# Four graph layers on eight batches: where the next pair's norm stands in the TensorE order of layer 3

## The chip, the cores and the metric

The kernel runs on one core of one Trainium2 chip. The metric is the device time of one execution in microseconds (us), taken as the median of several runs. The profile is of one more execution of the same kernel; its durations belong to that execution, whose own time is given beside its span below.

## The reference, cut to what matters

The input x has 8 batches of 2048 nodes with 64 features; adj is a 2048 x 2048 matrix of zeros and ones. Four layers follow one another, each of the form x + layer(relu(layernorm(x))). Only layers 2 and 3 and the norm matter for this change:

```python
def _layernorm(x, axis=-1, eps=1e-5):
    m = jnp.mean(x, axis=axis, keepdims=True)
    v = jnp.var(x, axis=axis, keepdims=True)
    return (x - m) / jnp.sqrt(v + eps)
...
    for _ in range(MAX_STEPS):                       # layer 2, three steps
        effects = jnp.einsum('nm,bmd->bnd', adj_matrix, v)
        h = jnp.concatenate([v, effects], axis=-1)
        h = jax.nn.relu(jnp.einsum('bnk,dk->bnd', h, W1) + b1)
        v = jnp.einsum('bnk,dk->bnd', h, W2) + b2
...
    As = [jnp.eye(N, dtype=x.dtype)]                 # layer 3
    As.append(A)
    for _ in range(2, K):
        As.append(2.0 * (A @ As[-1]) - As[-2])
    x_g = jnp.einsum('knm,bmc->bnkc', A_stack, x)
    out = jnp.einsum('bnki,nkio->bno', x_g, w)
```

So layer 2 multiplies by the adjacency three times, layer 3 twice more, and layer 3 ends with one product per node, whose weights come from 16 stored matrices mixed by an embedding of the node.

## The kernel before, in words

**Tiling.** Two batches make a pair, so that 2 x 64 features fill 128 partitions; there are NP = 4 pairs, done one after the other. The 2048 nodes are NT = 16 tiles of P = 128, or NCW = 4 chunks of CW = 512; the last chunk has the number LAST = 3. The adjacency lies in SBUF for the whole time, as 16 tiles aT[m].

**Spread.** The product with the adjacency is the function spread: for one chunk of 512 nodes it accumulates over all 16 source tiles m, two matmuls for each (a high and a low part of the operand), into one PSUM tile acc: 32 matmuls. For each pair there are 20 spreads: three steps of layer 2 with four chunks, then four chunks for each of layer 3's two products with the adjacency.

**Layer 3's products.** After the second spread of a chunk, its result is copied to y2 (L2113), and then come the products of that chunk: for each of its four node tiles k and each half w of the 16 weight matrices, matmuls of the 64-row halves of v, y1 and y2 with W3 into u0 and u1, two PSUM buffers each. That is 96 matmul records per chunk, "64*128" in the profile. VectorE multiplies each u by the embedding (L2135), adds the two halves w (L2139) and folds (L2146); GpSimd folds on and adds the residual xr (L2147 to L2149); the result is stored by SyncE's queue (L2150).

**The norm.** normed is a layernorm with relu across partitions. It has two TensorE products with the averaging matrix, mean and var, and between them the subtraction on VectorE (L1974) and the Square on ScalarE (L1975); after var come Ln and Exp (L1979, L1980) and the scaling on VectorE (L1981). enter is the norm of one chunk of the next pair's input, followed by moved: four small products py with W1e and their split in two parts (L1954, L1955). The last chunk has no free place in v, so it is normed in places of y1 that are no longer read, and copied to v at the pair's end (L2155).

**leave** ends layer 2 for one chunk: the product pv with W2, the residual (L2018), four transposes tx, the norm of layer 3 along the free dimension on VectorE and ScalarE (L2029 to L2040, its cast on ScalarE being L2039), and later the transposes tv. Before it, ScalarE's relu (L2084) has turned acc into v; pv reads that v.

**What sets the order.** Matmuls and transposes are kept in the order in which the program issues them (mm and turn, with strict on). Instructions of the other engines, and the loads on SyncE's queue, are put in order by the scheduler of the framework, which can take a later one first if it expects it to be ready first. The program's own order is written by Weave, a planner with a clock of its own: a chain is a generator that yields the delay to its next step, and a spread calls passed(0.47) after each source tile m, the products call passed(2.8) after each (k, w), and the first product of a layer 2 chunk passed(0.93). A step is issued at the first such call at which its due time is reached:

```python
    def passed(self, us):
        self.now += us
        for c in list(self.chains):
            if c[0] <= self.now:
                self.step(c)
```

In layer 3's loop over c, the chain enter(c - 1) is started after the second spread of chunk c and after the copy to y2, with a delay of 0.0; so its steps fall among the products of chunk c. With c = LAST there are two chains, for chunks 2 and 3. The chunk of the next pair's input is loaded ahead of the spread of chunk c; fin's tag x has two buffers, one of which holds xr. The mean and var of these chains use the PSUM buffers of acc. The last pair has no next one and no such chains.

Of the kernel before, what the change touches and what calls it, by code (L numbers as in the profile page):

```python
# [19 lines left out]
NP = B // 2  # L20
# [11 lines left out]
def cols(c, w=CW):  # L32
    return slice(c * w, (c + 1) * w)
# [1865 lines left out]
def layers23(self, aT):  # L1899
# [69 lines left out]
    def normed(dst, src, tags, xc=None):  # L1969

        mean = ps.tile([P, CW], FP, tag=tags[0], name="mean")
        mm(mean, kit.avg, src, start=True, stop=True)
        xc = fin.tile([P, CW], FP, tag="ca", name="xc") if xc is None else xc
        nc.vector.tensor_sub(xc, src, mean)  # L1974
        nc.scalar.activation(dst, xc, AF.Square)  # L1975
        yield 3.5
        var = ps.tile([P, CW], FP, tag=tags[1], name="var")
        mm(var, kit.avg, dst, start=True, stop=True)
        nc.scalar.activation(dst, var, AF.Ln, bias=kit.eps)  # L1979
        nc.scalar.activation(dst, dst, AF.Exp, scale=-0.5)  # L1980
        nc.vector.scalar_tensor_tensor(dst, xc, 0.0, dst, op0=OP.max, op1=OP.mult)  # L1981
        yield 3.5

    def spread(acc, y, c, start, ms):

# [11 lines left out]
    def chunk_of(src, c):  # L1997
        return load(fin.tile([P, CW], FP, tag="x", name="xp"), src, c)
# [13 lines left out]

    def leave(p, c, xp, yn):

        yield 1.4
        pv = ps.tile([P, CW], FP, tag="tp", name="pv")
        mm(pv, W2, v[:, cols(c)], start=True, stop=True)
        nc.vector.scalar_tensor_tensor(xp, pv, b2c, xp, op0=OP.add, op1=OP.add)  # L2018
        bq = load(sb.tile([P, CW], FP, tag="pr", name="bq", bufs=3), kit.bias_dram, c)
        yield 1.8  # L2020

        tx = ps.tile([P, 4, P], FP, tag="u0", name="tx")
        for k in range(4):
            kit.turn(tx[:, k, :], xp[:, k * P : (k + 1) * P])
        nc.scalar.copy(xp, tx.rearrange("p k n -> p (k n)"))  # L2025
        groups = lambda a: a.rearrange("p (g f) -> p g f", f=F)
        spans = lambda a: a[:, :, None].to_broadcast([P, 8, F])
        st = sb.tile([P, 2, 8], FP, tag="st", name="st")
        nc.vector.tensor_reduce(st[:, 0], groups(xp), AX.X, OP.add)  # L2029
        vn = fin.tile([P, CW], FP, tag="ca", name="vn")  # L2030
        nc.vector.scalar_tensor_tensor(groups(vn), spans(st[:, 0]), -1.0 / F, groups(xp), op0=OP.mult, op1=OP.add)
        nc.scalar.activation(v[:, cols(c)], vn, AF.Square)
        nc.vector.tensor_reduce(st[:, 1], groups(v[:, cols(c)]), AX.X, OP.add)
        nc.scalar.activation(st[:, 1], st[:, 1], AF.Ln, bias=kit.eps, scale=1.0 / F)
        nc.scalar.activation(st[:, 1], st[:, 1], AF.Exp, scale=-0.5)
        nc.vector.scalar_tensor_tensor(groups(vn), groups(vn), 0.0, spans(st[:, 1]), op0=OP.max, op1=OP.mult)
        hi, lo = parts(LENT[c])
        flat = lambda a: a.rearrange("p k n -> p (k n)")
        nc.scalar.copy(flat(hi), vn)  # L2039
        nc.vector.tensor_tensor(flat(lo), vn, flat(hi).bitcast(FP), op=OP.subtract)  # L2040
        yn[c] = hi, lo
        nc.gpsimd.tensor_add(bq, bq, xp)  # L2042
        nc.sync.dma_start(out=x3_dram[p, :, cols(c)], in_=bq)
        yield 7.0
        tv = ps.tile([P, 4, P], FP, tag="u1", name="tv")
        for k in range(4):
            kit.turn(tv[:, k, :], vn[:, k * P : (k + 1) * P])
        nc.scalar.copy(v[:, cols(c)], flat(tv))

    def again(y1, c, yn):  # L2050
        yield 1.4
        yn[c] = turned(y1, c)
# [17 lines left out]
    for p in range(NP):  # L2070
        for step in range(3):
            yn = [None] * NCW
            if p == 0 and step:
                weights(step)
            for c in range(NCW):
                acc = ps.tile([P, CW], FP, tag="acc", name="acc")
                if step < 2:
                    got = raw(2)
                else:
                    xp = chunk_of(x2_dram[p], c)  # L2080
                mm(acc, Wvc if step else W1v, v[:, cols(c)], start=True, stop=False)
                weave.passed(0.93)
                spread(acc, y, c, False, every)
                nc.scalar.activation(v[:, cols(c)], acc, AF.Relu, bias=b1c if step else b1)  # L2084
                if step < 2:
                    check(got)
                weave.start(carry(c, step, yn) if step < 2 else leave(p, c, xp, yn))
            y = yn


        y1 = sb.tile([P, N], FP, tag="y1", name="y1", bufs=1)
        yn, after = [None] * NCW, [None] * NCW

        two = [ps.tile([P, CW], FP, tag="acc", name="acc") for c in range(2)]
        for ms in (range(0, 8), range(8, 12), range(12, NT)):
            for c in range(2):
                spread(two[c], y, c, 0 in ms, ms)
                if NT - 1 in ms:
                    nc.scalar.copy(y1[:, cols(c)], two[c])
                    weave.start(again(y1, c, yn))  # L2100
        for c in range(2, NCW):
            acc = ps.tile([P, CW], FP, tag="acc", name="acc")
            spread(acc, y, c, True, every)
            nc.scalar.copy(y1[:, cols(c)], acc)
            weave.start(again(y1, c, yn))
        for c in range(NCW):
            xr = chunk_of(x3_dram[p], c)
            acc = ps.tile([P, CW], FP, tag="acc", name="acc")
            if c > 0 and p + 1 < NP:
                xp = chunk_of(x2_dram[p + 1], c - 1)  # L2110
            spread(acc, yn, c, True, every)
            y2 = fin.tile([P, CW], FP, tag="ca", name="y2")
            nc.scalar.copy(y2, acc)  # L2113
            if c > 0 and p + 1 < NP:
                weave.start(enter(c - 1, after, xp, 0.0, ("acc", "acc")))
                if c == LAST:

                    xp = load(y1[:, cols(0)], x2_dram[p + 1], c)
                    weave.start(enter(c, after, xp, 2.0, ("acc", "acc"), y1))
            for k in range(4):  # L2120
                i = 4 * c + k
                ns, ks = slice(i * P, (i + 1) * P), slice(k * P, (k + 1) * P)
                pr = []
                for w in range(2):
                    u = [ps.tile([P, 8, F], FP, tag=f"u{h}", name=f"u{h}") for h in range(2)]
                    for kk, src in enumerate((v[:, ns], y1[:, ns], y2[:, ks])):
                        for h in range(2):

                            mm(
                                u[h].rearrange("p d o -> p (d o)"), src[half(h), :], W3[half(h), kk, cols(w)],  # L2130
                                start=kk == 0, stop=kk == 2,
                            )
                    for h in range(2):
                        a = sb.tile([P, 8, F], FP, tag="pr", name="pr", bufs=3)
                        nc.vector.tensor_tensor(  # L2135
                            a, u[h], emb[:, i, 8 * w : 8 * w + 8, None].to_broadcast([P, 8, F]), op=OP.mult
                        )
                        if w:
                            nc.vector.tensor_add(pr[h], pr[h], a)  # L2139
                        else:  # L2140
                            pr.append(a)
                    weave.passed(2.8)
                fold = sb.tile([P, 2, 4, F], FP, tag="fold", name="fold")
                ot = sb.tile([P, 2, F], FP, tag="ot", name="ot", bufs=1)
                for h in range(2):
                    nc.vector.tensor_add(fold[:, h], pr[h][:, 0:4, :], pr[h][:, 4:8, :])  # L2146
                nc.gpsimd.tensor_add(fold[:, :, 0:2, :], fold[:, :, 0:2, :], fold[:, :, 2:4, :])  # L2147
                nc.gpsimd.tensor_add(ot, fold[:, :, 0, :], fold[:, :, 1, :])
                nc.gpsimd.tensor_add(ot, ot, xr[:, ks].rearrange("p (h f) -> p h f", h=2))  # L2149
                nc.sync.dma_start(  # L2150
                    out=out[2 * p : 2 * p + 2, ns, :].rearrange("h p f -> p h f"), in_=ot
                )
        if p + 1 < NP:
            weave.until(lambda: None not in after)
            nc.scalar.copy(v[:, cols(LAST)], y1[:, cols(1)])  # L2155
        y = after
# [103 lines left out]
```

## Time and profile before

| what | value |
| --- | --- |
| median of 3 runs (lowest, highest) | 1966.83 us (1963.56, 1970.12) |
| the profiled execution: its own time, its span | 1963.12 us, 1961.3 us |
| busy in the span: TensorE, VectorE, ScalarE, GpSimd | 1900.6, 1190.7, 438.0, 315.4 us |
| granted TensorE clock, mean | 0.989 |
| layers 2 and 3 of the four pairs | from about 862 us to the end |
| records of mean and var of the norms that enter makes (two for each product) | 24 and 24 |
| times that the loading of pv's weights waited for ScalarE's L2084 | 12, together 6.8 us |

The span is the time from the first to the last instruction; the execution's own time is 1.82 us longer. "Busy" counts instructions, not waits, and TensorE's matmuls are pipelined, so a matmul's own duration is longer than the step from one to the next. The step is read from the chain of work that ended last: there, consecutive matmuls of one kind are merged into one line with their number, and the length of the line divided by the number is the step. One product in full fp32 with 512 columns shows as two records.

### The profile page before, as it was taken

The numbers are of one execution on the slowest core, as the hardware profiler recorded it, in microseconds if no ns is written. First come the engines' busy times: TensorE is split into PE (matmuls) and PEld (weight loads), VectorE is DVE, ScalarE is ACT, GpSimd is POOL, SyncE is SP. The second block draws the span as 40 slices with busy tenths as digits, with TensorE's granted clock in tenths as the row PEclk, the third lists the DMA queues.
The fourth block names the chain that finished last, engine by engine and source line by source line (L and its number), as shares of the span: only waits on it lengthen the run. The fifth ranks groups of instructions, "written<-read, shape, count | busy, mean of one in ns | idle before, by whom it ended". The sixth has DMA issues, their size and how long they took to land.

```text
span 1961.3 us, 23490 instructions
## 1 busy us (share of the span) xinstructions
PE 1900.6 (97%) x9060; PEld 1134.5 (58%) x9060; DVE 1190.7 (61%) x1917; ACT 438.0 (22%) x923; POOL 315.4 (16%) x435
## 2 busy tenths in 40 slices
PE   7999999889999999999999999999999999999997
PEld 6877777423323232257775477764577755677653
DVE  8676499768999998953326642346623275523365
ACT  6322355573111110111210111301112201112100
POOL 4111177310000000000002110012200022101122
PEclk9999899999999999999999999999999999999998
DMA  7556485473221212223101011100122011121000
GB/s 216 168 177 178 134 235 147 113 187 76 55 54 46 64 38 60 60 55 83 60 11 30 27 58 54 49 17 24 31 65 59 22 25 30 44 70 49 3 21 12
DMA packets 86362, 142.43 MB, mean 73 GB/s; under 512 B 33800, under 2 KB 34056, under 8 KB 83568
## 3 DMA queue, kind: packets, MB, share of 16 engines
q1 hardware_dynamic: 65200, 83.86, 14.3%
q0 software_dynamic: 21040, 56.98, 11.9%
q8 instruction: 73, 1.20, 0.3%
q14 instruction: 49, 0.40, 0.1%
HBM read 106.85 MB, written 37.09 MB: 73 GB/s over the span
## 4 chain that ended last, share of the span: by engine, by line
PE 66%; issue 17%; DVE 6%; DMA 4%; ACT 3%; POOL 3%; SPq 0%; POOLq 0%; DVEq 0%; ACTq 0%
PE acc L734 28%; PE u L734 14%; PE o L734 4%; PE py L734 3%; PE pd L734 2%; PE dn L734 2%; PE pgs L734 2%; PE acc L1058 2%; DMA at<-in_adjT 1%; PE var L734 1%; PE mean L734 1%; DMA den<-d_dram 1%; PE pv L734 1%; PE pf L734 1%; PE pm L734 1%
## 5 line engine op out<-in xcount | busy, mean ns | idle before, releaser
L734 PE MATMUL acc<-aT,parts 128*128 128x512 f32 x1664 | 448.2, 415 | 0.0
L734 PEld LDWEIGHTS acc<-aT,parts 128*128 128x128 f32 x1664 | 306.5, 188 | 102.2 <-issue 39.8
L2135 DVE TENSOR_TENSOR pr<-u,embf 128x512 f32<-128x512 f32 x256 | 170.7, 688 | 171.2 <-PE u L734 163.5
L734 PE MATMUL u<-W3f,y 64*128 64x512 f32 x1024 | 243.3, 589 | 0.0
L1733 DVE SCALAR_TENSOR_TENSOR pt<-R,wd,aT 128x1024 f32<-128x1024 f32 x192 | 236.2, 1280 | 9.5 <-DMA R<-r_dram 4.5
L734 PE MATMUL o<-pt,hS 128*64 128x512 f32 x1024 | 237.5, 599 | 0.8 <-DVE pt L1733 0.6
L734 PEld LDWEIGHTS u<-W3f,y 64*128 64x128 f32 x1024 | 101.8, 187 | 118.6 <-issue 118.6
L734 PEld LDWEIGHTS o<-pt,hS 128*64 128x64 f32 x1024 | 68.3, 136 | 160.2 <-issue 149.5
L734 PE MATMUL u<-W3f,v 64*128 64x512 f32 x512 | 137.9, 607 | 0.0
L2147 POOL TENSOR_TENSOR fold<-fold 128x256 f32<-128x256 f32 x64 | 47.7, 746 | 506.3 <-DVE fold L2146 506.3
L734 PE MATMUL dn<-pt,vd 128*32 128x512 f32 x1024 | 123.1, 598 | 0.0
L1952 DVE TENSOR_TENSOR yb<-py,cb_f 128x512 f32<-128x512 f32 x32 | 22.1, 691 | 161.4 <-PE py L734 161.4
L1058 PE MATMUL acc<-at,Y 128*128 128x512 f32 x384 | 105.1, 416 | 0.0
L734 PE MATMUL acc<-aTl,parts 128*128 128x512 f32 x384 | 96.5, 393 | 0.0
L2042 POOL TENSOR_TENSOR bq<-bq,xp 128x512 f32<-128x512 f32 x16 | 20.6, 1287 | 432.7 <-ACT xp L2025 432.7
L2139 DVE TENSOR_TENSOR pr<-pr 128x512 f32<-128x512 f32 x128 | 88.2, 689 | 2.2
L1733 DVE SCALAR_TENSOR_TENSOR pt<-R,wd,aTl 128x1024 f32<-128x1024 f32 x64 | 79.8, 1282 | 12.4 <-PE dn L734 8.2
L734 PEld LDWEIGHTS u<-W3f,v 64*128 64x128 f32 x512 | 51.4, 186 | 56.1 <-issue 34.1
L734 PEld LDWEIGHTS acc<-aTl,parts 128*128 128x128 f32 x384 | 72.1, 188 | 16.9
L1058 PEld LDWEIGHTS acc<-at,Y 128*128 128x128 f32 x384 | 70.6, 194 | 14.7 <-issue 1.3
L734 PEld LDWEIGHTS dn<-pt,vd 128*32 128x32 f32 x1024 | 26.9, 108 | 80.9 <-issue 77.1
L2113 ACT COPY y<-acc 128x512 f32<-128x512 f32 x16 | 9.4, 585 | 279.7 <-PE acc L734 279.7
(354 smaller groups left out, 2697.0 us busy)
## 6 DMA issues: line engine op xcount, KB each, us to landing
at<-in_adjT POOLq DMA_DIRECT2D x32, 512.0 KB, 5.5
raw<-in_adjT SPq DMA_DIRECT2D x64, 256.0 KB, 3.4
aT<-in_adjT POOLq DMA_DIRECT2D x12, 1024.0 KB, 5.5
xp<-xd SPq DMA_DIRECT2D x45, 256.0 KB, 3.0
R<-r_dram SPq DMA_DIRECT2D x14, 512.0 KB, 3.7
hlo<-lo_dram POOLq DMA_DIRECT2D x18, 235.1 KB, 3.9
hhi<-hi_dram POOLq DMA_DIRECT2D x18, 235.1 KB, 3.4
hi_dram<-hi SPq DMA_DIRECT2D x16, 264.0 KB, 3.4
```

Of the source, the lines that this page charges most:

```text
L734: one = self.nc.tensor.matmul(*args, **kw)
L1058: mm(acc[p], Y[h][:, m, p, :], at[:, k, :], start=m + h == 0, stop=m == NT - 1 and h == 1)
L1733: nc.vector.scalar_tensor_tensor(pt, R[b2], wd[:, m, b2 : b2 + 1], aT[m][:, s].bitcast(FP), op0=OP.max, op1=OP.mult)
L1952: nc.vector.tensor_tensor(yb, py, bias[:, None, :].to_broadcast([P, 4, P]), op=OP.add)
L2042: nc.gpsimd.tensor_add(bq, bq, xp)
L2113: nc.scalar.copy(y2, acc)
L2135: nc.vector.tensor_tensor(a, u[h], emb[:, i, 8 * w : 8 * w + 8, None].to_broadcast([P, 8, F]), op=OP.mult)
L2139: nc.vector.tensor_add(pr[h], pr[h], a)
L2147: nc.gpsimd.tensor_add(fold[:, :, 0:2, :], fold[:, :, 0:2, :], fold[:, :, 2:4, :])
```

## The change

- In normed the delay after each half goes from 3.5 to 3.0.
- In leave the delay ahead of pv goes from 1.4 to 2.3, and to 1.8 for the last chunk.
- In layer 3's loop the load of the next pair's chunk c is issued after the second spread of chunk c (it was ahead of the next spread), for c up to 2; the load of the last chunk into y1 is issued with c = 2 (it was with c = 3).
- enter(c - 1) is started ahead of the second spread of chunk c instead of after it, with a delay of 0.2; for c = 3 the chain of the last chunk is started with it, with a delay of 0.6 (it was 2.0).
- The mean and var of these chains use the PSUM buffers of u0 and u1 instead of those of acc.

```diff
@@ normed @@
-        yield 3.5
+        yield 3.0
         var = ps.tile([P, CW], FP, tag=tags[1], name="var")
...
-        yield 3.5
+        yield 3.0
@@ leave @@
-        yield 1.4
+        yield 1.8 if c == LAST else 2.3
         pv = ps.tile([P, CW], FP, tag="tp", name="pv")
@@ layers23, the loop over c that ends layer 3 @@
+        xn = None
         for c in range(NCW):
             xr = chunk_of(x3_dram[p], c)
             acc = ps.tile([P, CW], FP, tag="acc", name="acc")
-            if c > 0 and p + 1 < NP:
-                xp = chunk_of(x2_dram[p + 1], c - 1)
+            if xn is not None:
+                weave.start(enter(c - 1, after, xn, 0.2, ("u0", "u1")))
+                if c == LAST:
+                    weave.start(enter(c, after, xl, 0.6, ("u0", "u1"), y1))
             spread(acc, yn, c, True, every)
             y2 = fin.tile([P, CW], FP, tag="ca", name="y2")
             nc.scalar.copy(y2, acc)
-            if c > 0 and p + 1 < NP:
-                weave.start(enter(c - 1, after, xp, 0.0, ("acc", "acc")))
-                if c == LAST:
-
-                    xp = load(y1[:, cols(0)], x2_dram[p + 1], c)
-                    weave.start(enter(c, after, xp, 2.0, ("acc", "acc"), y1))
+            if c < LAST and p + 1 < NP:
+                xn = chunk_of(x2_dram[p + 1], c)
+                if c == LAST - 1:
+                    xl = load(y1[:, cols(0)], x2_dram[p + 1], LAST)
```

## The prediction

> **What bounds the kernel now.** I read the page first: the busy line and the shares of the chain that ended last.
>
> ```profile
> PE 1900.6 (97%) x9060; PEld 1134.5 (58%) x9060; DVE 1190.7 (61%) x1917; ACT 438.0 (22%) x923; POOL 315.4 (16%) x435
> PE 66%; issue 17%; DVE 6%; DMA 4%; ACT 3%; POOL 3%; SPq 0%; POOLq 0%; DVEq 0%; ACTq 0%
> ```
>
> TensorE sets the end, so the change is worth what it takes from TensorE's sequence. The matmuls are the same before and after; only switches and waits between them can go. "97% busy" can't show those, because modelled matmul ends cover small gaps. So next I read the chain of waits piece by piece, where a piece divided by its count gives the step from matmul to matmul. Second pair, layer 3, chunks 0 and 1 (start, length, what):
>
> ```profile
> 1292.17 20.81 PE u L734 x96
> 1312.98 7.66 PE acc L734 x32
> 1320.63 2.78 PE u L734 x12
> 1323.41 1.06 PE mean L734 x2
> 1324.46 5.35 PE u L734 x24
> 1329.82 1.05 PE var L734 x2
> 1330.87 5.35 PE u L734 x24
> 1336.22 1.09 PE py L734 x8
> 1337.31 7.93 PE u L734 x36
> ```
>
> Chunk 0 runs its 96 u in one piece. Chunk 1 has them in four pieces of 21.41 us together, 0.60 more, though there is no engine's wait between them. Third, the end of layer 2 in the same pair:
>
> ```profile
> 1213.15 8.32 PE acc L734 x34
> 1221.47 0.86 PE pv L734 x2
> ...
> 1229.98 0.62 ACT parts L2039
> 1230.60 0.60 ACT v L2084
> 1231.24 1.12 PE pv L734 x2
> ```
>
> The first pv costs 0.86. For the second the chain leaves TensorE: pv waits for v from L2084, and that relu stood behind the cast L2039 on ScalarE. The list of waits has this 12 times (6.8 us of PEld): chunks 1, 2, 3 of four pairs. Fourth, the timeline at the start of chunk 1's spread, for who is busy where the norm is to go:
>
> ```profile
> 1312.91 5.87 PE L734 MATMUL acc<-aT,parts 128*128 128x512 f32 x24
> ...
> 1313.85 0.39 SPq L1994 DMA_DIRECT2D y<-xd  x1
> 1314.52 0.69 DVE L2135 TENSOR_TENSOR pr<-u,embf 128x512 f32<-128x512 f32 x1
> 1315.13 0.41 DVE L2146 TENSOR_TENSOR fold<-pr 128x256 f32<-128x256 f32 x1
> 1315.46 0.69 DVE L2139 TENSOR_TENSOR pr<-pr 128x512 f32<-128x512 f32 x1
> 1316.18 0.42 DVE L2146 TENSOR_TENSOR fold<-pr 128x256 f32<-128x256 f32 x1
> ```
>
> VectorE is still in chunk 0's products until 1316.60, S + 3.7 (S is the spread's start, 1312.91); ScalarE is free. A fold runs before an add that the program has ahead of it, and y's load, which the program has in chunk 3, runs in chunk 1: outside TensorE the scheduler does take what it expects to be ready.
>
> **What the Trainium skill says.** "TensorEngine Tiling (Array Packing)", Key Properties: changing the tiling mode drains TensorE. The trace agrees in size: the u are "64*128", mean, var and py "128*128", and each of the six changes in a chunk costs about 0.2 us. "TensorE: Matmul & The Clock Gate", section on the architectural detail of the array: matmuls stay in program order, ScalarE and VectorE are strict first-in first-out. The trace agrees: L2084 starts at the end of L2039's stretch although its acc was done. "Perfetto Trace Analysis", Tensor Engine Instruction: the profiler estimates a matmul's end. Hence the chain's steps and not durations here.
>
> **The change part by part.**
>
> *1. The norms leave the products.* In chunk 1, from 1320.63 to 1345.24 are 24.61 us with one norm; without one, 20.81: it costs 3.80. In the spread there is no mode change: a product of two records with 512 columns costs 0.86 there (pv above; also the first product of a layer 2 chunk, 8.32 for 34 records against 7.46 for 32), and eight py 0.89, as read in layer 2's spreads. So 0.86 + 0.86 + 0.89 = 2.61, a gain of 1.19 for the chunk, as for chunk 2. Chunk 3 with two norms: 27.21 - 20.81 = 6.40 against 5.22, a gain of 1.18. The sum is 3.56 for a pair, and three pairs have a next one: **10.7 us**. Neither end of this is much open: 1.06 for mean or var holds the mode change, and less than 0.86 is seen nowhere. VectorE's share (0.69 for each of L1974, L1981, L1955) leaves the products too, but chunk 0 shows that TensorE then runs at 20.81 and no faster, so I count nothing for it.
>
> *2. New waits in the spread.* By the planner, mean comes after the first m, var seven m later (7 x 0.47 reaches 3.0), py seven later again: 15 of 16 m. With 3.5 it would be eight, and 17. A spread's m takes 0.466 us. So mean is at S + 0.6, and var at 0.6 + 0.86 + 7 x 0.466 = S + 4.7. Behind var, if it waits, the whole spread is queued. What it needs: L1974 on VectorE (0.68), then the Square (0.63). If L1974 goes behind the whole tail of the products, it runs from S + 3.7 to 4.4, the Square to 5.05: a wait of 0.35. If the scheduler puts it into the gap ahead of the last fold, at about S + 3.2, there is none. From var to L1981's end the trace shows 3.2 us (1329.75 to 1332.98), and py comes 0.86 + 3.26 = 4.1 later: none. Chunk 3 has mean, m, mean ahead and so var at about S + 5.6: none. The bounds are 0 and 6 x 0.35 = 2.1 us (chunks 1, 2 of three pairs); below 0 is excluded, as a wait can't give time. I take **0.6 lost**. PSUM: mean takes the older u0 buffer, whose reader L2135 was done before S; in chunk 3 the second mean (S + 1.9) and var take the newer ones, read by S + 1.6 + 0.7. At the end ScalarE has the cast of py and the copy to y2 (0.58 each); products need y2 only eight records (1.7 us) in, so it hides.
>
> *3. Loads.* SyncE's queue gets the same loads, earlier. Each waits for the previous L1974 (now early in the spread) and has a whole chunk of some 28 us for 3.0 us of landing; stores ahead of it only wait for GpSimd. The load into y1 already ran in chunk 1. Cost 0, hidden by the products; uncovered, see the third rival.
>
> *4. pv later.* By the planner pv stood one m after the first product (0.93 + 0.47 reaches 1.4), now three (2.34 reaches 2.3); for chunk 3 the fourth m instead of the third. Cost now: from tx to tx the chain has 1224.19, 1234.67, 1245.12, 1255.57, so 10.48, 10.45, 10.45. TensorE's own work is 0.86 + 7.46 + 0.86 + 0.45 + 0.45 = 10.08, and 10.15 in the third (36 records, no first product): 0.40 + 0.37 + 0.30 = 1.07 lost in a pair, 4.3 in four. Does it go? tx moves with pv, and so does L2039: if L2084 stays behind it, the circle tx, L2039, L2084, pv keeps its 10.45, and only chunk 3, where the next pv moves one m and not two, gains 4 x 0.3 = 1.2. But now L2039's input is ready some 0.9 us after L2084's instead of in a tie, and L2084 takes 0.69; a scheduler that goes by readiness puts the relu first. Then v is there 1.0 after the spread, pv wants it at 2.3, and all goes. Bounds 1.2 and 4.3; I take **4.3**. tv moves along behind pv; layer 3 needs the last chunk's parts some 1.4 us after they are ready, so nothing is late there.
>
> *Sum:* -10.7 + 0.6 - 4.3 = -14.4. Against the profiled execution (1963.12; span 1961.3 plus 1.82 around it) that is 1948.7. The median is 3.71 above the profiled execution; the same subtraction gives **1952.4**.
>
> **The rivals.**
>
> *Waits stay.* L2084 stays behind L2039 and L1974 goes behind the tail: -10.7 - 1.2 + 2.1 = -9.8, 1957.0. For it: both engines keep their order once it is set, and in before the cast did go first. Against: the scheduler's order by readiness seen above.
>
> *The spread swallows it.* The norm in the spread waits about 0.9 us each time (VectorE's tail later than in chunk 0, 1381.46 being S + 4.1 in chunk 3's spread, and L1974, Square and var in turn): -10.7 - 1.2 + 9 x 0.9 = -3.8, 1963.0, no measurable change. Against: that late tail came from the norm in the products, which is gone.
>
> *The load comes late (slower).* If SyncE's queue has the load behind the chunk's last store (1318.52, S + 5.6), it lands at about S + 9.0, and mean, wanted at S + 0.6, holds TensorE for 8.4 us in nine spreads: +76 - 15 = +61, 2028. It decides from 15.0 / 9 = 1.7 us a spread, a landing after S + 2.3. Against: the program issues the load ahead of the chunk's stores, and its buffer is free long before.
>
> **How the numbers follow.** Forecast 0.67, waits stay 0.23, swallowed 0.06, late load 0.04. Best bounds: 10.7 + 4.3 + 0.7 (two odd pieces of u, 21.16 and 8.27, that may not recur) = 15.7, 1951.1; the first rival ends at 1957.0. The runs lie 3.3 either side of their median; I allow some 2.5 for a median: 1948.5 to 1960, leaving out the last two cases, 0.10. A measurement of this kernel tells about 0.3% (5.9 us) from no change: faster 0.90, same 0.06, slower 0.04.
>
> **What would show it.** Right: in pairs 1 to 3 every chunk's 96 u in one piece of 20.8; mean and var at 0.86 inside the spreads, which grow by 2.6 (5.2 in chunk 3); L2084 ahead of L2039 on ScalarE, tx to tx at 10.1, no pv waiting for L2084. Wrong: var pieces well over 0.9 with L1975 in the chain; pv still at 1.12; a mean that waits for a DMA; u pieces that stay above 20.8.

## The result, and the profile after

The changed kernel takes 1952.55 us (median of 5 runs, 1951.52 to 1955.08) against 1967.05 us for the kernel before (5 runs, two more than in the table ahead, 1963.56 to 1970.12): 14.5 us less, ratio 0.992 with a 95% interval of 0.9901 to 0.9939. The forecast was 1952.4, or 14.4 less.

The page's busy line and chain shares:

```profile
PE 1888.2 (97%) x9060; PEld 1141.7 (58%) x9060; DVE 1191.2 (61%) x1917; ACT 437.4 (22%) x923; POOL 310.3 (16%) x435
PE 74%; issue 14%; DVE 4%; DMA 3%; POOL 3%; ACT 1%; SPq 0%; POOLq 0%; DVEq 0%; ACTq 0%
```

The counts of instructions are those of before, and TensorE is as full as before at 97%. But its share of the chain rose from 66% to 74%, and ScalarE's fell from 3% to 1%, VectorE's from 6% to 4%: the ends of layer 2 have left the chain. Now the chain piece by piece, second pair, layer 3, chunks 0 and 1 (start, length, what):

```profile
1292.02 20.81 PE u L734 x96
1312.83 0.66 PE acc L734 x2
1313.48 0.86 PE mean L734 x2
1314.34 3.28 PE acc L734 x14
1317.62 0.86 PE var L734 x2
1318.48 3.25 PE acc L734 x14
1321.72 0.89 PE py L734 x8
1322.61 0.47 PE acc L734 x2
1323.08 20.81 PE u L734 x96
```

All 96 u of chunk 1 are in one piece of 20.81, as in chunk 0. The norm's products stand in the spread at 0.86, 0.86 and 0.89; the pieces of acc between them keep their 0.233 a matmul (a matmul's own duration in the timeline is 0.39). The first two acc take 0.66 instead of 0.47, as they follow the u: that change of row mode was there before too, in the 7.66 for 32. From the first u of this pair to the end of its last are 116.62 us, against 120.17 (1292.17 to 1412.34) before. The other pairs with a next one: 116.97 against 120.50, 116.63 against 120.51. Sum: 10.96 us.

The end of layer 2 in the same chain:

```profile
1223.41 0.86 PE pv L734 x2
1224.27 1.86 PE acc L734 x8
1226.13 0.44 PE tx L741 x4
1226.57 6.44 PE acc L734 x26
1233.01 0.86 PE pv L734 x2
...
1236.18 0.44 PE tx L741 x4
```

No piece of ScalarE or VectorE is left in it, pv takes 0.86 in chunk 1 too, and from tx to tx there are 10.05, 10.04 and 9.66 us (10.48, 10.45, 10.45 before; the last interval now has one source tile fewer). The timeline shows why:

```profile
1230.59 1.02 PE L734 MATMUL acc<-v,Wvc_f 128*128 128x512 f32 x2
1231.08 0.67 ACT L2084 ACTIVATE v<-acc,b1c_f 128x512 f32<-128x512 f32 x1
1231.21 0.69 DVE L2036 SCALAR_TENSOR_TENSOR vn<-vn,st 128x512 f32<-128x512 f32 x1 [0.61 <-ACT st L2035]
1231.93 0.62 ACT L2039 CAST parts<-vn 128x512 fp32r<-128x512 f32 x1 [0.18 <-DVE vn L2036]
1232.85 1.02 PE L734 MATMUL pv<-v,W_f 128*128 128x512 f32 x2
```

The relu L2084 now goes first. It is done at 1231.75, while VectorE still makes the cast's input, and pv asks for v only at 1232.85.

**The two profiled executions differ by less than the medians.** They took 1963.12 and 1953.49 us, 9.6 apart. That is a difference in layers 0 and 1, which the change does not touch: the first product of layer 2 (acc from v and W1v) starts at 862.8 before and at 868.6 after. From there to the end of the span there are 1098.5 and 1083.1 us, 15.4 apart. This stretch, "layers 2 and 3" in the table, is used below beside the times. Each kernel has one profile, so how well the stretch repeats is seen only from kernels that should agree in it: 1087.4 and 1087.3 us, and 1093.7 and 1093.8, while single times of one kernel lie up to 15.7 us apart.

### The profile page after: what moved, and what is told of

Read it like the earlier page. It is cut to its first block, busy times and chain, and to the rows that moved or that the text cites. A ratio compares the mean times of both kernels' runs of the same rounds, so it can differ in the third digit from the quotient of the medians.

```text
span 1951.7 us, 23508 instructions
## 1 busy us (share of the span) xinstructions
PE 1888.2 (97%) x9060; PEld 1141.7 (58%) x9060; DVE 1191.2 (61%) x1917; ACT 437.4 (22%) x923; POOL 310.3 (16%) x435
## 4 chain that ended last, share of the span: by engine, by line
PE 74%; issue 14%; DVE 4%; DMA 3%; POOL 3%; ACT 1%; SPq 0%; POOLq 0%; DVEq 0%; ACTq 0%
PE acc L734 33%; PE u L734 13%; PE o L734 6%; PE dn L734 3%; PE py L734 3%; PE pgs L734 2%; PE acc L1058 2%; PE pd L734 2%; PE var L734 1%; PE mean L734 1%; DMA iv<-ind_dram 1%; DMA at<-in_adjT 1%; DVE pt L1733 1%; PE pv L734 1%; PE pm L734 1%
## 5 line engine op out<-in xcount | busy, mean ns | idle before, releaser
L734 PE MATMUL acc<-aT,parts 128*128 128x512 f32 x1664 | 462.0, 421 | 0.0
L2140 DVE TENSOR_TENSOR pr<-pr 128x512 f32<-128x512 f32 x128 | 88.2, 689 | 2.2
L2042 POOL TENSOR_TENSOR bq<-bq,xp 128x512 f32<-128x512 f32 x16 | 20.6, 1289 | 430.1 <-ACT xp L2025 430.1
L734 PEld LDWEIGHTS u<-W3f,v 64*128 64x128 f32 x512 | 57.3, 186 | 49.6 <-issue 36.1
L1966 DVE TENSOR_TENSOR parts<-tp,parts 128x512 fp32r<-128x512 f32 x16 | 11.1, 692 | 85.7 <-ACT parts L1965 85.7
```

Of the source, the lines that this page charges most:

```text
L734: one = self.nc.tensor.matmul(*args, **kw)
L1966: nc.vector.tensor_tensor(lo, tp, hi.bitcast(FP), op=OP.subtract)
```

## The experiments

My theory had three parts: a change between 128-row and 64-row products costs TensorE about 0.2 us, and the norm in the products made six of them in a chunk; pv waited because the relu stood behind the cast on ScalarE; the two are independent. The rivals were waits for other engines in place of the mode changes, and pv's mere lateness in place of ScalarE's order.

| kernel | median us (runs) | ratio to before, 95% interval | layers 2 and 3, us | products of pair 2, us | tx to tx, pair 2 |
| --- | --- | --- | --- | --- | --- |
| before | 1967.05 (5) | | 1098.5 | 120.17 | 10.48, 10.45, 10.45 |
| changed | 1952.55 (5) | 0.992 (0.9901 to 0.9939) | 1083.1 | 116.62 | 10.05, 10.04, 9.66 |
| norm alone | 1955.02 (6) | 0.9934 (0.9912 to 0.9956) | 1087.4 | 116.61 | 10.48, 10.45, 10.45 |
| pv alone | 1963.18 (14) | 0.9988 (0.9972 to 1.0004) | 1093.7 | 120.17 | 10.04, 10.05, 9.65 |
| changed, cast first | 1959.35 (14) | 0.9961 (0.9947 to 0.9975) | 1089.4 | 116.63 | 10.49, 10.44, 10.44 |
| before, relu first | 1960.44 (15) | 0.9964 (0.9953 to 0.9975) | 1093.8 | 120.18 | 10.03, 10.04, 10.11 |
| changed, pv one tile later only | 1956.38 (10) | 0.9953 (0.9937 to 0.9969) | 1087.3 | 116.59 | 10.49, 10.43, 10.46 |
| changed, delay 3.5 | 1957.22 (6) | 0.9941 (0.9918 to 0.9963) | 1086.5 | 117.83 | 10.05, 10.04, 9.65 |
| extra product among the 64-row ones | 1971.5 (20) | 1.0023 (1.001 to 1.0036) | 1102.6 | 121.63 | 10.05, 10.04, 9.65 |
| the same in two halves of 64 rows | 1962.33 (10) | 0.9968 (0.9952 to 0.9984) | 1096.4 | 120.02 | 10.04, 10.05, 9.65 |
| the same in the spread | 1966.12 (20) | 0.999 (0.9976 to 1.0005) | 1096.6 | 119.18 | 10.04, 10.05, 9.66 |
| two chunks at once | 1948.33 (6) | 0.9908 (0.9889 to 0.9926) | 1080.4 | other order | 10.05, 10.05, 9.65 |

Each ratio was taken against runs of the kernel before on the same chip. For effects of a few us out of 1967 the ratios give the direction at best (two of the intervals, pv alone and the product in the spread, hold 1); the sizes are read from the stages.

**The norm alone.** pv's delay is put back in the changed kernel:

```diff
-        yield 1.8 if c == LAST else 2.3
+        yield 1.4
```

> The changed kernel with the delay ahead of pv put back to 1.4 for every chunk, so that only the norm has moved. My theory (the norm gains by mode changes saved, pv by the order on ScalarE, and the two are independent): the products of the second pair, from its first u to the end of its last, take 116.6 us as in the changed kernel (120.2 before), and tx to tx is 10.45, 10.45, 10.45 as before; 1952.6 + 4.3 = 1956.9 us, ratio 0.995. Rival (the gain of the products depends on pv's place, or is not there alone): products above 118.

The products of the second pair take 116.61, tx to tx is 10.48, 10.45, 10.45 again, and layers 2 and 3 take 1087.4: 11.1 below before and 4.3 above the changed kernel. The rival's "above 118" is out. The norm's part stands alone.

**pv alone.** The same line, new in the kernel before.

> The kernel before with the new delays ahead of pv (2.3, and 1.8 for the last chunk) and nothing else. My theory: tx to tx falls from 10.48, 10.45, 10.45 to 10.05, 10.05 and 9.68 (the last one has one source tile fewer between its two tx), the products stay at 120.2; 1967.0 - 4.3 = 1962.7 us, ratio 0.998. Rival (part of this gain comes from the freed products): tx to tx stays above 10.2.

tx to tx is 10.04, 10.05, 9.65, the products stay at 120.17, layers 2 and 3 are 4.8 shorter. The two parts give 11.1 + 4.8 = 15.9 against 15.4 together: independent, to within 0.5 us. The time alone does not show pv's part, as its interval holds 1; the stage and the tx do.

**Cast first.** Everything of the change stays, pv's place too; only ScalarE's order is set back:

```diff
-        nc.scalar.copy(flat(hi), vn)
+        tc.keep_in_program_order(nc.scalar.copy(flat(hi), vn))
...
-                nc.scalar.activation(v[:, cols(c)], acc, AF.Relu, bias=b1c if step else b1)
+                tc.keep_in_program_order(nc.scalar.activation(v[:, cols(c)], acc, AF.Relu, bias=b1c if step else b1))
```

> The changed kernel, with ScalarE's cast L2039 and relu L2084 kept in the order in which the program issues them, so that the cast goes first as in the kernel before; pv stays where the change put it. My theory (pv waits because the relu stands behind the cast): tx to tx is 10.45, 10.45 again and about 9.9 for the last, pv pieces of 1.1 us return in chunks 1 to 3, and the time is 3 us above the changed kernel, 1955.6. Rival (a later pv gives v time, whatever ScalarE's order): tx to tx stays 10.05 and 9.66, 1952.6 us.

The chain of this kernel, second pair, chunk 1:

```profile
1232.90 0.62 ACT parts L2039
1233.53 0.60 ACT v L2084
1234.12 0.04 issue
1234.17 1.13 PE pv L734 x2
...
1237.60 0.45 PE tx L741 x4
```

ScalarE is back in the chain, and so is a pv of 1.1 in every chunk from 1 to 3 of the four pairs, though pv stands as late as in the changed kernel. The rival is out. The size missed: layers 2 and 3 are 6.3 longer than in the changed kernel, not 3. I had expected about 9.9 for the last tx to tx; it is 10.44, like the others. The circle of tx, L2039, L2084 and pv takes its 10.45 whatever TensorE has to do meanwhile, and in the last interval it has only 9.66.

**Relu first.** The reverse, in the kernel before, with pv where it was. The cast, with the subtraction that follows it, becomes a step of its own that the program issues after the next relu, and cast and relu are kept in that order:

```diff
+        nc.gpsimd.tensor_add(bq, bq, xp)
+        nc.sync.dma_start(out=x3_dram[p, :, cols(c)], in_=bq)
+        yield 5.2
         hi, lo = parts(LENT[c])
         flat = lambda a: a.rearrange("p k n -> p (k n)")
-        nc.scalar.copy(flat(hi), vn)
+        tc.keep_in_program_order(nc.scalar.copy(flat(hi), vn))
         nc.vector.tensor_tensor(flat(lo), vn, flat(hi).bitcast(FP), op=OP.subtract)
         yn[c] = hi, lo
-        nc.gpsimd.tensor_add(bq, bq, xp)
-        nc.sync.dma_start(out=x3_dram[p, :, cols(c)], in_=bq)
-        yield 7.0
+        yield 0.9
...
-                nc.scalar.activation(v[:, cols(c)], acc, AF.Relu, bias=b1c if step else b1)
+                tc.keep_in_program_order(nc.scalar.activation(v[:, cols(c)], acc, AF.Relu, bias=b1c if step else b1))
```

> The kernel before, pv at its old place (1.4), but the cast L2039 with its subtraction is issued as a step of its own 5.2 later, after the next chunk's relu, and the two are kept in that order on ScalarE; the transposes tv stay at their place, one source tile earlier for one chunk. My theory (the order on ScalarE is the cause): pv takes 0.86 in all chunks without having moved, tx to tx is about 10.1, and the time is 4.3 us below the kernel before, 1962.7. Rival (pv must come later for v to be ready): pv stays at 1.1 and tx to tx at 10.45, 1967.0 us.

In its timeline, second pair (the edit shifts the lines: the relu is L2085 here, the cast L2042):

```profile
1236.97 0.69 ACT L2085 ACTIVATE v<-acc,b1c_f 128x512 f32<-128x512 f32 x1 [0.56 <-PE acc L734]
1237.56 0.61 ACT L2042 CAST parts<-vn 128x512 fp32r<-128x512 f32 x1
1238.10 1.02 PE L734 MATMUL pv<-v,W_f 128*128 128x512 f32 x2
```

pv takes 0.86 in the chain in all 16 places without having moved; tx to tx is 10.03, 10.04, 10.11, and layers 2 and 3 are 4.7 shorter than before. The order on ScalarE is enough; a later pv isn't needed.

**pv one tile later only.** In the changed kernel the delay is 1.8 for every chunk.

> The changed kernel with a delay of 1.8 ahead of pv for every chunk, so one source tile later than before instead of two for the first three. In this kernel the scheduler leaves the cast L2039 ahead of the relu L2084 on ScalarE. My theory (the order decides, and tx moves with pv): nothing is gained against the old place, tx to tx 10.45 three times, pv 1.1 in chunks 1 to 3, 4.3 us above the changed kernel, 1956.9. Rival (each later source tile gives v 0.47 us more): the wait of 0.3 is covered, tx to tx 10.1, 1952.6 us.

The timeline of this kernel, second pair, chunk 1:

```profile
1227.68 1.02 PE L734 MATMUL acc<-v,Wvc_f 128*128 128x512 f32 x2
1227.84 0.69 DVE L2036 SCALAR_TENSOR_TENSOR vn<-vn,st 128x512 f32<-128x512 f32 x1 [0.61 <-ACT st L2035]
1228.56 0.62 ACT L2039 CAST parts<-vn 128x512 fp32r<-128x512 f32 x1 [0.76 <-DVE vn L2036]
1229.09 0.68 ACT L2084 ACTIVATE v<-acc,b1c_f 128x512 f32<-128x512 f32 x1
1229.82 1.13 PE L734 MATMUL pv<-v,W_f 128*128 128x512 f32 x2 [0.19 <-ACT v L2084]
```

The cast is still first, tx to tx is 10.49, 10.43, 10.46, and layers 2 and 3 take 1087.3, the same as with pv at its old place (1087.4). A later pv by itself gains nothing. The change's delay of 2.3 works because with the second source tile the scheduler put the relu first. Why it did so with two tiles and not with one is not shown. By an estimate from the traces the relu's input was ready first here as well: in the kernel with the relu first, the relu that waited for its acc started 0.2 us after the next chunk's first product (1236.97 after 1236.77). Here that would be 1227.9, and the cast's input was ready only at 1228.53, when L2036 ended.

**Delay 3.5 in normed.** Both lines `yield 3.0` are 3.5 again.

> The changed kernel with the delays in normed put back to 3.5: var then comes one source tile later, and the products py fall after the first (k, w) of the chunk's products instead of into the spread. My theory (each product that stands between the 64-row products costs two mode changes, 0.2 us each): every chunk with a norm has its u in two pieces again, a chunk costs 0.4 more, also the last with its two py side by side, 9 x 0.4 = 3.6 us, 1956.2. Rival (a py is as cheap in the products): 1952.6 and u in one stretch of 20.8 plus 0.9.

The chain of this kernel, second pair, from the start of chunk 1's spread:

```profile
1318.11 0.67 PE acc L734 x2
1318.78 0.86 PE mean L734 x2
1319.64 3.75 PE acc L734 x16
1323.38 0.86 PE var L734 x2
1324.24 3.27 PE acc L734 x14
1327.51 2.77 PE u L734 x12
1330.28 1.09 PE py L734 x8
1331.37 18.23 PE u L734 x84
```

py misses the spread by one source tile, costs 1.09 instead of 0.89 itself, and the u take 21.00 instead of 20.81. The pair's products grow by 117.83 - 116.62 = 1.21 for three chunks, 0.40 each; layers 2 and 3 by 3.4.

**An extra product, three ways.** In the changed kernel, one product more in each of the 16 chunks; nobody reads its result, so no engine is waited for. First 128 rows among the 64-row products:

```diff
+                    if k == 1 and w == 0:
+                        ex = ps.tile([P, CW], FP, tag="tp", name="ex")
+                        mm(ex, kit.avg, y2, start=True, stop=True)
                     weave.passed(2.8)
```

> The changed kernel with one more product of 128 rows (the averaging matrix with y2, 512 columns, two records) in the middle of each chunk's products, 16 in all; its result is not used. No wait and no other engine is in it. My theory (mode changes): it takes 1.06 itself and 0.2 more for the u after it, a chunk grows by 1.26, 16 x 1.26 = 20.2 us, 1972.7. Rival (the u were split by waits for other engines, the change of mode is free): 16 x 0.86 = 13.8 us, 1966.3.

Then the same in two halves, `mm(ex, kit.avg[half(h), :], y2[half(h), :], ...)` for h = 0 and 1:

> As the kernel with the extra product of 128 rows, but it is cut into two products of 64 rows each (four records of 64*128), the same mode as the products around it; the results are not used. My theory: no change of mode, four records at 0.2147 us, a chunk grows by 0.86, 13.7 us in all, 1966.3, although it has more records than the uncut one. Rival (any foreign product in the stream costs 0.4 more): 16 x 1.26 = 20.2 us, 1972.7.

And the first one with y1 as its operand, between the source tiles 7 and 8 of the second spread:

> The changed kernel with the same extra product of 128 rows, put in the middle of each of the 16 second spreads of layer 3 (with y1 as its operand; its result is not used). My theory: 0.86 each, 13.8 us in all, 1966.3: some 6 us less than the same product among the 64-row products. Rival (a product in full fp32 costs more in the spread too): 1.26 each, 1972.7.

Chunk 0 of the second pair, first with the full product, then with the halves:

```profile
1293.77 7.93 PE u L734 x36
1301.69 1.06 PE ex L734 x2
1302.75 13.08 PE u L734 x60
```

```profile
1296.65 7.93 PE u L734 x36
1304.57 0.86 PE ex L734 x4
1305.43 12.88 PE u L734 x60
```

The u are split in both, but only the 128-row product makes what follows it longer (13.08 against 12.88) and is itself 0.2 longer. A pair's products grow by 5.01 for four chunks with the full product (1.25 each), by 3.40 with the halves (0.85 each), and by 2.56 for the three spreads of that stretch (0.85 each) with the product in the spread. Layers 2 and 3 grow by 19.5, 13.3 and 13.5 us. So one product in the wrong mode costs 0.40 us more for its place; it isn't the split, and there is no wait in it. Nor is it the step from one element type to another: in the spread the same full fp32 product stands among fp32r ones and costs nothing beyond its 0.86. The medians agree in order (19.0, 9.8, 13.6 above the changed kernel), the second only roughly.

**Two chunks at once.** If the changes of mode are what costs, fewer stretches of products must be faster. The loop is regrouped; xn has a buffer of its own, and chunk 1's input is loaded into a free place of y1:

```diff
-        for c in range(NCW):
+        for cs in ((0, 1), (2,), (3,)) if more else ((0, 1), (2, 3)):
+            for c in cs:
...
+                spread(acc, yn, c, True, every)
...
+            for c in cs:
+                xr, y2 = xrs[c], y2s[c]
                 for k in range(4):
```

> A version that follows from the theory of mode changes: layer 3's second spreads of chunks 0 and 1 run one after the other, then the products of both, and in the last pair also those of chunks 2 and 3; the norms of the next pair's chunks 0 and 1 run in the spread of chunk 2, those of 2 and 3 in the spread of chunk 3. All work stays. It saves one leaving and one entering of the 64-row mode in pairs 1 to 3 and two in the last, 5 x 0.4 = 2.0 us. My theory: products of the second pair 116.2 instead of 116.6, 1950.6 us in all. Rival (the changes at the spread's start are hidden behind VectorE, or two norms in chunk 2's spread wait): products of 116.6 or more, 1952.6 or more.

```profile
1288.12 13.52 PE acc L734 x58
1301.64 41.41 PE u L734 x192
1343.05 0.67 PE acc L734 x2
1343.71 0.86 PE mean L734 x2
```

The u of two chunks take 41.41 instead of 2 x 20.81 = 41.62, and the second spread starts without its own 0.2. From one pair's end to the next (1141.18 to 1410.41) are 269.23 us, against 269.71 in the changed kernel (1138.93 to 1408.64): 0.48 less, where 0.4 was forecast. The mean and var of both norms in chunk 2's spread take 0.86 each, so the rival's waits did not come. Layers 2 and 3 take 1080.4, 2.7 less. The median, 1948.33, is the lowest of all, but its interval overlaps that of the changed kernel: the gain over it is shown by the stages and not by the times.

## Why the prediction was right, point by point

**1. The norms leave the products: right.** 10.7 us were worked out and 10.96 measured in the three pairs; 0.34 of it is an odd piece of u (8.27 before, in the third pair) that did not recur; the other odd piece, 21.16, is there as before. Each price held: 0.86, 0.86, 0.89 in the spread, 20.81 for the u. That the 0.60 us in the pieces of u were changes of mode and not waits was only argued then; the extra product in one piece and in halves shows it. The prediction's "agrees in size" had no size to agree with: the 0.2 us for one change is these traces' own figure.

**2. New waits in the spread: inside the bounds, on the good side.** I gave 0.6 for var, with 0 to 2.1 as bounds. It was 0. The start of chunk 1's spread (the change shifts the lines of the products by one: here the add is L2140 and the fold L2147):

```profile
1312.76 0.72 PE L734 MATMUL acc<-aT,parts 128*128 128x512 f32 x2
...
1315.32 0.69 DVE L2140 TENSOR_TENSOR pr<-pr 128x512 f32<-128x512 f32 x1
1315.92 0.68 DVE L1974 TENSOR_TENSOR xc<-xp,mean 128x512 f32<-128x512 f32 x1
1316.51 0.42 DVE L2147 TENSOR_TENSOR fold<-pr 128x256 f32<-128x256 f32 x1
1316.63 0.63 ACT L1975 ACTIVATE v<-xc 128x512 f32<-128x512 f32 x1 [23.99 <-DVE xc L1974]
...
1317.46 1.02 PE L734 MATMUL var<-v,avg_f 128*128 128x512 f32 x2
```

L1974 went into the gap ahead of the last fold, at S + 3.2, and var comes at S + 4.7, both as worked out. The Square ends at 1317.26, 0.2 us before var. Behind the fold, some 0.4 later, it would have been late. The cover is thin: it holds because of one place in VectorE's order, and that the scheduler would choose this place was a guess. Nothing else of the norm waits in the spread either: in all three pairs the 14 acc between mean and var take 3.26 to 3.28 us, and the two acc ahead of a chunk's first mean 0.65 to 0.67, so no mean waits for its u buffer.

**3. Loads: right.** No mean waits for a transfer; the load of chunk 1 is issued at 1316.63, as soon as L1974 has freed its buffer, a chunk ahead of its use. No run moved the loads or the PSUM buffers alone.

**4. pv later: right in the value taken, wrong in a bound.** 4.3 were taken, and the part alone gave 4.8: TensorE's own 10.08 was 10.05, and the last interval lost its 0.3 of waiting as said. The reason given, that a scheduler which goes by readiness puts the relu first, isn't shown: with one source tile the relu's input was ready first too, by the estimate above, and it still went second. So the order turned as forecast, but partly by luck. And I had set the other end at a gain of 1.2, "only chunk 3, where the next pv moves one m and not two, gains". Had the order on ScalarE stayed, it would have been a loss: the kernel with the cast first has pv late and takes 1089.4 us in layers 2 and 3, against 1087.4 for the norm alone, which has the cast first as well and pv at its old place: 2.0 us more. The step that failed is that a smaller move of chunk 3's pv would shorten the last interval. All of the circle is latency, its 10.45 doesn't depend on where pv stands, so TensorE, with one source tile (0.47 us) less to do in that interval, waits 0.47 longer. Over four pairs that is 1.9 us. This rival would have ended near 1960 and not at 1957.0.

**Sum.** -14.4 forecast, -15.4 in layers 2 and 3 of the two profiled executions, -14.5 between the medians. That the medians agree with the forecast to 0.1 us is luck: the waits of part 2 were put 0.6 too high and pv's part 0.5 too low, and the runs of one kernel lie several us apart. None of the three rivals came.

## What to carry to other kernels

Where TensorE sets the end and is "97% busy", divide the chain's pieces by their counts: a product in another row mode cost its own time and some 0.4 us of changes here, so put it where its mode already runs, in a stretch where the engines it needs are idle. Before moving an instruction that waits, follow the circle that its result closes: if that is all latency, as here, moving it gains nothing (1087.3 us against 1087.4), and the order on the slow engine (here one relu ahead of one cast) is what has to change. Compare stages and not only totals when another stage scatters more than the change is worth.

## What the runs showed of the hardware that was not expected

The prediction did not use this, and the expectation of the run had it right: four records of 64 rows (0.86 us) are as cheap among 64-row products as two records of 128 rows in the spread (0.86), and cheaper than those two among the 64-row ones (1.06, and 0.20 more for the next u).

In the profiled executions the scatter comes from ahead of layer 1's norm, which the change doesn't touch. In the twelve of them layer 2 starts between 860.6 and 872.6 us, and layer 1's norm between 458.4 and 469.1, so nearly all of the spread is there by then. It goes roughly with the mean TensorE clock granted between 200 and 460 us: 0.94 to 0.95 in the three executions that start layer 2 at 860.6, 862.8 and 865.6, 0.93 in the five from 864.7 to 870.8, 0.91 in the four at 868.1 and from 871.1 to 872.6. Whether the clock is the cause, and why it differs there, was not tried.
